# A 1x1 convolution's first image by seven half-size products for eight, in a two-layer convolution kernel on one core

## The chip, the cores and the metric

The kernel runs on one core of a Trainium2 chip. A core has a matrix engine (TensorE, PE in the profile), a vector engine (VectorE, DVE), a scalar engine (ScalarE, ACT), a general engine (GpSimd, POOL) and a queue engine (SyncE, SP). Each takes its instructions in order; they wait for each other on semaphores. DMAs are issued from SP, ACT or POOL. The metric is the device time of one execution in microseconds, lower is better.

## The reference

The input x has 4 images of 1024 channels and 56 x 56 pixels, float32. Two layers follow each other. The change is in the first line of the first layer, for the first image.

```
# layer 0
r = relu(conv1x1(x, w1) + b1)                 # 1024 -> 256 channels
off = conv3x3(r, w_off) + b_off               # 18 offsets a pixel
s = bilinear samples of r at 9 taps moved by off
r = relu(einsum(s, w2) + b2)                  # 256 -> 256
x = relu(x + conv1x1(r, w3) + b3)             # 256 -> 1024
# layer 1
out = relu(bn(conv1x1(x, w1)))                # 1024 -> 256, statistics over the batch
out = relu(bn(conv3x3(out, w2)))
out = bn(conv1x1(out, w3))                    # 256 -> 1024
return relu(x + softplus(residual_scale) * out)
```

## The kernel before

Channels lie on the 128 partitions, pixels along the free axis. An image is cut into 7 blocks of 8 rows, 448 pixels (BLK), which stage_a takes one by one. For block j of image n:

- load_x (L252, L254) loads x in four pieces of 256 channels into the pool xin, which has four buffers. So a piece for the next block is loaded when the same piece of this block has been used.
- The first product (L266) is 8 groups of input channels by 2 halves of output channels, 16 matmuls 448 wide, into acc, a PSUM tile of two banks with one buffer. Each float32 matmul is two instructions in the profile, so that a block shows 32.
- Two ScalarE operations (L278) read acc, add the bias, apply relu and write feat.
- From the third block on, stage_b of the block two before comes in between: po (L355) turns the offsets on PE, and 16 small VectorE operations (L368 to L390) make sampling weights and indices.
- pm (L292) is the offset convolution, part (L301) its copy by VectorE, and six small DMAs (L309) on SP bring it into offc.
- ftp (L322) turns feat on PE, three ScalarE copies (L329 to L332) fill ft, and four DMAs (L336, L340) on SP store it into the image's table in memory, twice, for two corners of a sample.

When image 0 has all seven blocks, its sampling begins: an indirect DMA on GpSimd (L405) gathers rows of the table into one of the eight buffers g of the pool gat, ScalarE (L415) and VectorE (L417) mix four corners, PE turns the result (stp, L439) and multiplies it (L455). From here on the blocks of the next image and the last products (stage_c, L480 and L507) are woven in by a budget of columns. Image 0's blocks have nothing to be woven with; they run one after another, followed by image 1's first product.

The kernel is written against a scheduling layer: it places buffers, orders each engine's instructions by its own estimates, and puts in the semaphore waits. Two details matter here. The order on an engine need not be that of the source. And every DMA from SP or ACT takes one of eight semaphores in turn, so that a DMA can be issued only when an earlier one with the same semaphore has landed.

Of the kernel before, what the change touches and what calls it, by code (L numbers as in the profile page):

```python
# [8 lines left out]
F32 = mybir.dt.float32  # L9
I32 = mybir.dt.int32  # L10
AF = mybir.ActivationFunctionType
ALU = mybir.AluOpType

N, CIN, H, W = 4, 1024, 56, 56
CB = 256
KC = CIN // 128
KB = CB // 128
HW = H * W
ROWS = 8
BLK = ROWS * W  # L20
NJ = H // ROWS
# [17 lines left out]
R2S = 5  # L39
X1S = 6  # L40
# [20 lines left out]
def deform_bottleneck_then_bn_bottleneck(  # L61
# [15 lines left out]
    nc = tc.nc  # L77
# [23 lines left out]
    def col(name, k):  # L101
        c = COLS[name] + k
        return ch[:, c : c + 1]
# [64 lines left out]
    with ExitStack() as l0:  # L168
# [4 lines left out]
        xin = l0a.enter_context(tc.tile_pool(name="xin", bufs=4, side="right"))  # L173
        worka = l0a.enter_context(tc.tile_pool(name="work_a", bufs=2, side="right"))
        xres = l0.enter_context(tc.tile_pool(name="xres", bufs=2))
        gat = l0.enter_context(tc.tile_pool(name="gat", bufs=8))
        work = l0.enter_context(tc.tile_pool(name="work", bufs=2))
        w3p = l0.enter_context(tc.tile_pool(name="work3", bufs=3))
        per_image = l0.enter_context(tc.tile_pool(name="per_image", bufs=2))
        ps1 = l0.enter_context(tc.tile_pool(name="ps1", bufs=4, space=bass.MemoryType.PSUM))  # L180
        ps2 = l0.enter_context(tc.tile_pool(name="ps2", bufs=1, space=bass.MemoryType.PSUM))

        w1 = wa.tile([128, KC, CB], F32, tag="w1", name="w1")
# [12 lines left out]
        def load_later():  # L196
            nc.sync.dma_start(w2, a_w2.rearrange("(h p) t o -> p h t o", p=128))
            nc.sync.dma_start(w3, a_w3.rearrange("(h p) o -> p h o", p=128))
            nc.sync.dma_start(c1w, b_w1.rearrange("(k p) o -> p k o", p=128))
# [26 lines left out]
        def load_zeros():  # L226
            zero = w3p.tile([128, CB], F32, tag="s", name="zero", bufs=12)
            nc.vector.memset(zero[: PW + 2], 0.0)
            for n in range(N):
                for corner, s in enumerate((0, PW)):  # L230
                    first_row = PW - s + TPAD
                    for r0, r1 in ((0, first_row), (first_row + H * PW, TROWS)):
                        if r1 > r0:
                            nc.sync.dma_start(tables[n][r0:r1, corner, :], zero[: r1 - r0, :])

        feats = []
        for i in range(2):
            f = wa.tile([128, KB, ROWS, PW], F32, tag=f"feat{i}", name=f"feat{i}")
# [7 lines left out]
        xts = {}  # L246

        def load_x(n, j, kk):
            if n == N:
                return  # L250
            if (n, j) == (0, 0):
                nc.sync.dma_start(w1[:, kk : kk + 2], w1_v[:, kk : kk + 2])  # L252
            xt = xin.tile([128, 2, BLK], F32, tag="xt", name=f"xt_{n}_{j}_{kk}")
            nc.sync.dma_start(xt, x_v[n, :, kk : kk + 2, j * BLK : (j + 1) * BLK])  # L254
            xts[n, j, kk] = xt

        def stage_a(n, j):

            b = n * NJ + j
            acc = ps2.tile([128, KB, 512], F32, tag="wide", name=f"acc1_{b}")
            for k in range(KC):
                xt = xts.pop((n, j, k)) if k % 2 == 0 else xt
                for h in range(KB):
                    nc.tensor.matmul(  # L266
                        acc[:, h, :BLK],
                        w1[:, k, h * 128 : (h + 1) * 128],
                        xt[:, k % 2, :],
                        start=(k == 0),  # L270
                        stop=(k == KC - 1),
                    )
                if k % 2:
                    load_x(*((n, j + 1) if j + 1 < NJ else (n + 1, 0)), k - 1)
                yield KB * BLK
            f = feats[b % 2]
            for h in range(KB):
                nc.scalar.activation(  # L278
                    f[:, h, :, 1 : 1 + W],
                    acc[:, h, :BLK].rearrange("p (r w) -> p r w", w=W),  # L280
                    AF.Relu,
                    bias=col("a_b1", h),
                )
            if j > 1:
                yield from stage_b(n, j - 2)
            yield None


            pm = ps1.tile([128, BLK], F32, tag="bank", name=f"pm_{b}")
            for kj in range(3):  # L290
                for h in range(KB):
                    nc.tensor.matmul(  # L292
                        pm[64 * h : 64 * h + 64, :],
                        woff[:, h, kj, :],
                        f[:, h, :, kj : kj + W],
                        start=(kj == 0),
                        stop=(kj == 2),
                    )
            yield 3 * BLK
            part = worka.tile([128, BLK], F32, tag="part", name=f"part_{b}")  # L300
            nc.vector.tensor_copy(part, pm)  # L301

            for ki in range(3):
                y0, y1 = ROWS * j + 1 - ki, ROWS * (j + 1) + 1 - ki
                lo, hi = max(y0, 0), min(y1, H)
                for h in range(KB):
                    to = (3 * h + ki) * OFFS
                    at = 64 * h + ki * OFFS
                    nc.sync.dma_start(  # L309
                        offc[to : to + OFFS, lo * W : hi * W],  # L310
                        part[at : at + OFFS, (lo - y0) * W : (hi - y0) * W],
                    )

            ft = worka.tile([128, QFULL + 1, CB], F32, tag="ft", name=f"ft_{b}")
            for half in range(2):
                tp = ps1.tile([128, 2, CB], F32, tag="bank", name=f"ftp_{b}_{half}")
                for i in range(2):
                    t = 2 * half + i
                    m = 128 if t < QFULL else QREST
                    for h in range(KB):  # L320
                        fv = f[:, h].rearrange("p r w -> p (r w)")
                        nc.tensor.transpose(  # L322
                            tp[:m, i, h * 128 : (h + 1) * 128],
                            fv[:, t * 128 : t * 128 + m],
                            ident,
                        )
                yield CB
                if half == 0:
                    nc.scalar.copy(ft[:, 0:2, :], tp)  # L329
                else:  # L330
                    nc.scalar.copy(ft[:, 2, :], tp[:, 0, :])
                    nc.scalar.copy(ft[:QREST, 3, :], tp[:QREST, 1, :])  # L332
            q = PW * (ROWS * j + 1)
            for corner, s in enumerate((0, PW)):
                r = q - s + TPAD
                nc.sync.dma_start(  # L336
                    tables[n][r : r + QFULL * 128, corner, :].rearrange("(t p) c -> p t c", p=128),
                    ft[:, :QFULL, :],
                )
                nc.sync.dma_start(  # L340
                    tables[n][r + QFULL * 128 : r + QB, corner, :], ft[:QREST, QFULL, :]
                )

# [257 lines left out]
        for kk in range(0, KC, 2):  # L601
            load_x(0, 0, kk)
# [13 lines left out]
        for j in range(NJ):  # L616
            for _ in stage_a(0, j):
                pass
            if j == 1:
                load_later()  # L620
            if j == 3:
                load_zeros()
# [20 lines left out]
        def next_stage(n, passed):  # L643
            if first_ones and first_ones[0][0] == n + 1:
                if first_ones[0][1] <= passed * (NJ + 1) or not last_ones:
                    running.append(stage_a(*first_ones.pop(0)))
                    return running[-1]
            if last_ones:
                return stage_c(*last_ones.pop(0))
            return None  # L650
# [50 lines left out]
    with l1:  # L701
# [8 lines left out]
        v, vs = [], []  # L710
        for p in range(6):
            t = wino.tile([128, QUADS, KB, PW], F32, tag=f"v{p}", name=f"v{p}")
# [273 lines left out]
        for i, p in [(i, p) for i in range(len(parts)) for p in SEQ] + [(len(parts), None)]:  # L986
            begun = begin(i, p) if p is not None else None
            if before is not None:
                j, q, _ = before
# [19 lines left out]
    ps2 = ctx.enter_context(tc.tile_pool(name="ps2_l1", bufs=1, space=bass.MemoryType.PSUM))  # L1009
# [30 lines left out]
    with ExitStack() as l2:  # L1040
# [46 lines left out]
        first = ps1.tile([128, 512], F32, tag="bank", name="first")  # L1087
        for h in range(KB):
# [4 lines left out]
                start=True,  # L1093
                stop=True,
# [5 lines left out]
        for i in range(0, len(chunks), 2):  # L1100
            n, at, m = chunks[i + 1]
# [71 lines left out]
    for n in range(N):  # L1173
        for j in range(NJ):
            blk = slice(j * BLK, (j + 1) * BLK)
            for kk in range(0, KC, 2):
                x1t = fin.tile([128, 2, BLK], F32, tag="x1f", name=f"x1f_{n}_{j}_{kk}")
                nc.sync.dma_start(x1t, x1_v[n, :, kk : kk + 2, blk])
                last = (n, j, kk) == (N - 1, NJ - 1, KC - 2)
                for d in range(2):  # L1180
                    k = kk + d
# [68 lines left out]
```

## Time and profile before

| | us |
|---|---|
| median of 3 runs | 2911.69 |
| lowest, highest | 2909.29, 2919.39 |
| the profiled execution | 2925.49 |
| its span, first to last instruction | 2923.6 |
| mean granted clock of TensorE | 0.990 of full |

The profile counts from the span's start. PE is busy for 98% of it and VectorE for 64%. The stretches below are block by block; the columns are the stretch, its length, then the busy time and number of instructions of PE, of weight loads on PE, of VectorE, ScalarE and GpSimd, then PE's granted clock, the DMA engines' busy share and GB/s.

```profile
0.00:25.16 25.16, 17.85 (x52) 9.04 (x53) 10.24 (x49) 4.37 (x7) 0.79 (x7) 1.00 0.83 295
25.16:41.93 16.77, 16.04 (x54) 8.16 (x53) 0.63 (x1) 2.28 (x6) 0.00 (x0) 1.00 0.71 236
41.93:58.76 16.83, 16.42 (x58) 8.63 (x57) 3.58 (x16) 2.24 (x6) 0.00 (x0) 1.00 0.73 242
58.76:75.60 16.84, 16.43 (x59) 8.64 (x58) 3.58 (x16) 2.29 (x6) 0.00 (x0) 1.00 0.60 186
75.60:95.49 19.89, 16.58 (x58) 8.56 (x57) 3.58 (x16) 3.21 (x8) 0.00 (x0) 1.00 0.52 170
95.49:114.05 18.56, 18.14 (x57) 9.46 (x58) 3.58 (x16) 1.35 (x3) 0.00 (x0) 0.91 0.69 218
114.05:130.88 16.83, 16.33 (x57) 8.54 (x56) 3.32 (x16) 2.28 (x6) 0.00 (x0) 1.00 0.57 177
130.88:147.71 16.83, 12.19 (x34) 5.89 (x32) 0.50 (x2) 2.60 (x6) 5.23 (x6) 0.97 0.72 226
```

Each stretch is one block of image 0, from one first product's start to the next; the last holds image 1's first product and the start of the sampling. Matmuls overlap in their pipeline, and a record of one is longer (0.55 us at 448 wide) than the time from one to the next. A lone matmul's record is thus no measure of the pace.

### The profile page before, as it was taken

Reading aid. Unit: us, or ns where it says so; the run is one execution under the profiler, and the core shown is the slowest. Engines: PE = TensorE matmul, PEld = TensorE weight load, DVE = VectorE, ACT = ScalarE, POOL = GpSimd, SP = SyncE. Lnnn points to the kernel's source line nnn. Section 1 sums busy time; section 2 is a strip of 40 time slices with the busy share of each in tenths; the row PEclk is TensorE's granted clock in tenths of the full one; section 3 lists DMA queues with packets and bytes.
Section 4 is the critical chain, followed back from the end, with each engine's and each line's share of the span. In section 5 each row is a group of like instructions: output and inputs, shape, how many; then the busy total and the mean of one; then the engine's idle time right before and its main releaser. Section 6 shows DMA issues by size and latency. Waiting matters only on the chain. (4 is left out here: it accounts for less than half of the span.)

```text
span 2923.6 us, 34375 instructions
## 1 busy us (share of the span) xinstructions
PE 2852.8 (98%) x10473; PEld 1700.7 (58%) x10473; DVE 1884.1 (64%) x4257; ACT 1188.6 (41%) x2439; POOL 1029.2 (35%) x998
## 2 busy tenths in 40 slices
PE   8899999999999999999999899999989998999999
PEld 4444455565554555555555455545669998965554
DVE  2188676676566667666676786767659887344444
ACT  1144443444334444344344344444434544334444
POOL 0065554456445546555554654444300000000000
PEclk9999999999999999999999999999999999999999
DMA  7699999898898999888897999999731101049997
GB/s 249 192 382 387 334 330 318 301 357 313 301 339 304 337 300 347 313 316 327 321 337 232 366 324 311 333 334 320 234 101 46 46 23 64 14 159 311 308 308 261
DMA packets 330331, 789.49 MB, mean 270 GB/s; under 512 B 31352, under 2 KB 176800, under 8 KB 329888
## 3 DMA queue, kind: packets, MB, share of 16 engines
q0 software_dynamic: 127296, 462.48, 44.4%
q1 hardware_dynamic: 172368, 273.41, 27.8%
q10 hardware_dynamic: 30480, 51.39, 4.7%
q8 instruction: 83, 1.36, 0.2%
q14 instruction: 104, 0.85, 0.1%
HBM read 639.11 MB, written 142.70 MB: 267 GB/s over the span
## 5 line engine op out<-in xcount | busy, mean ns | idle before, releaser
L405 POOL DMA_INDIRECT g<-table,idxs x900 | 1018.3, 1131 | 1080.8 <-DVE s L417 550.9
L417 DVE SCALAR_TENSOR_TENSOR s<-g,wts,s 128x256 f32<-128x256 f32 (+1 forms) x2700 | 1134.1, 478 | 344.3 <-ACT s L415 326.7
L455 PE MATMUL acc<-sts,w 128*128 128x512 f32 (+2 forms) x2016 | 809.0, 543 | 0.6 <-ACT r L465 0.6
L415 ACT ACTIVATE s<-g,wts 128x256 f32<-128x256 f32 x900 | 417.7, 509 | 469.4 <-PE stp L439 370.6
L455 PEld LDWEIGHTS acc<-sts,w 128*128 128x128 f32 x2016 | 363.0, 191 | 281.4 <-issue 197.4
L507 PE MATMUL pr<-r,w 128*128 128x512 f32 (+2 forms) x896 | 371.0, 545 | 13.0 <-DVE x1t L514 6.6
L480 PE MATMUL acc<-x1t,c1w 128*128 128x512 f32 (+2 forms) x896 | 370.1, 542 | 5.7 <-ACT x1t L517 5.7
L266 PE MATMUL acc<-xt,w 128*128 128x448 f32 x896 | 355.0, 547 | 14.1 <-DMA xt<-in_x_dram 9.5
L1018 PE MATMUL pf<-y,c3w 128*128 128x448 f32 x844 | 317.4, 539 | 0.0
L517 ACT ACTIVATE x1t<-x1t 128x512 f32<-128x512 f32 (+2 forms) x224 | 128.7, 575 | 446.2 <-DVE x1t L514 430.9
L514 DVE SCALAR_TENSOR_TENSOR x1t<-pr,ch,xr 128x512 f32<-128x512 f32 (+2 forms) x224 | 151.9, 681 | 226.8 <-PE pr L507 169.0
L439 PEld LDWEIGHTS stp<-ident,s 128*128 128x128 f32 (+1 forms) x1800 | 213.8, 142 | 139.6 <-issue 89.0
L266 PEld LDWEIGHTS acc<-xt,w 128*128 128x128 f32 x896 | 170.5, 193 | 173.7 <-issue 161.3
L480 PEld LDWEIGHTS acc<-x1t,c1w 128*128 128x128 f32 x896 | 171.2, 191 | 171.7 <-issue 117.3
L507 PEld LDWEIGHTS pr<-r,w 128*128 128x128 f32 x896 | 170.4, 192 | 172.5 <-issue 105.1
L439 PE MATMUL stp<-ident,s 128*128 128x128 f32 (+1 forms) x1800 | 248.1, 274 | 9.8 <-ACT sts L445 4.7
L445 ACT COPY sts<-stp 128x512 f32<-128x512 f32 (+2 forms) x504 | 243.1, 527 | 33.6 <-PE stp L439 33.6
L1182 DVE SCALAR_TENSOR_TENSOR x1f<-pf,sc_bn,x1f 128x448 f32<-128x448 f32 x211 | 144.3, 684 | 172.4 <-PE pf L1018 147.0
L1018 PEld LDWEIGHTS pf<-y,c3w 128*128 128x128 f32 x844 | 160.4, 190 | 156.8 <-issue 118.9
L1190 ACT ACTIVATE x1f<-x1f,sh_bn 128x448 f32<-128x448 f32 x224 | 148.3, 667 | 173.7 <-DVE x1f L1182 172.8
L845 PE MATMUL q<-v,u 128*128 128x196 f32 x576 | 109.5, 337 | 10.9 <-DVE v L797 9.7
L845 PEld LDWEIGHTS q<-v,u 128*128 128x128 f32 x576 | 99.4, 191 | 15.6 <-ACT y L762 10.2
(195 smaller groups left out, 1754.4 us busy)
## 6 DMA issues: line engine op xcount, KB each, us to landing
xt<-in_x_dram SPq DMA_DIRECT2D x112, 448.0 KB
x1f<-x_d SPq DMA_DIRECT2D x112, 448.0 KB
out_dram<-x1f ACTq DMA_DIRECT2D x111, 448.0 KB
xr<-in_x_dram SPq DMA_DIRECT2D x64, 512.0 KB
x_d<-x1t SPq DMA_DIRECT2D x128, 256.0 KB
table<-ft SPq DMA_DIRECT2D x56, 384.0 KB
g<-table,idxs POOLq DMA_INDIRECT x900, 7.2
xr<-in_x_dram SPq DMA_DIRECT2D x32, 384.0 KB
```

The costliest lines, as they stand in the source:

```text
L266: nc.tensor.matmul(acc[:, h, :BLK], w1[:, k, h * 128 : (h + 1) * 128], xt[:, k % 2, :], start=(k == 0), stop=(k == KC - 1),)
L405: nc.gpsimd.indirect_dma_start(out=g[:m], out_offset=None, in_=tables[n].rearrange("r q c -> r (q c)"), in_offset=bass.IndirectOffsetOnAxi ...
L415: nc.scalar.activation(s[:m], g[:m, 0:CB], AF.Copy, scale=wt[:, 0])
L417: nc.vector.scalar_tensor_tensor(s[:m], g[:m, corner * CB : (corner + 1) * CB], wt[:, corner], s[:m], ALU.mult, ALU.add,)
L439: nc.tensor.transpose(banks[h][:, t * 128 : t * 128 + m], s[:m, h * 128 : (h + 1) * 128], ident[:m, :m],)
L445: nc.scalar.copy(sts[:, h, :size], banks[h][:, :size])
L455: nc.tensor.matmul(acc[:, o, :size], w2[:, h, k, o * 128 : (o + 1) * 128], sts[:, h, :size], start=(k == 0 and h == 0), stop=(k == TAPS - ...
L480: nc.tensor.matmul(acc3[:, h, :size], c1w[:, k, h * 128 : (h + 1) * 128], x1t, start=(k == 0), stop=(k == KC - 1),)
L507: nc.tensor.matmul(pr, w3[:, h, k * 128 : (k + 1) * 128], r2[:, h, :size], start=(h == 0), stop=(h == KB - 1),)
L514: nc.vector.scalar_tensor_tensor(x1t, pr, col("a_b3", k), xr[:, d, :], ALU.add, ALU.add)
L845: nc.tensor.matmul(ps[:, o].rearrange("p r c -> p (r c)"), wt, x, start=first and j == 0 and (alone or o == 0), stop=last and j == len(pai ...
L1018: nc.tensor.matmul(pz, c3w[:, h, k * 128 : (k + 1) * 128], y2[n][:, h, j * BLK : (j + 1) * BLK], start=(h == 0), stop=(h == KB - 1),)
```

## The change

For blocks 1 to 6 of image 0 the first product is split in halves: the 8 groups of input channels into two times 4, the 256 output channels into two times 128, and the 448 pixels into two times 224. Eight products of half sizes become seven, by Winograd's form of Strassen's scheme: four sums of weights, made once by VectorE after the first block, and four sums of x a block, eight VectorE instructions of 448 elements. The seven products, 4 matmuls 224 wide each, go into three places of acc: y and z in one bank, v in the other. ScalarE reads a partial result of y or v into feat between products (keep), VectorE adds another one to it (finish), and ScalarE applies relu. Block 0 and the other images keep 16 matmuls.

With it, image 0's x goes into the eight buffers of the samples (gat), so that a block's x is loaded while the block before is computed, and the table stores of image 0 are issued from ScalarE's queue and no longer from SP's. The sums of x lie in buffers of r2, the sums of weights in buffers of x1t, both unused until image 0's samples are multiplied.

```diff
-            xt = xin.tile([128, 2, BLK], F32, tag="xt", name=f"xt_{n}_{j}_{kk}")
+            if n == 0:
+                xt = gat.tile([128, 4 * CB], F32, tag="g", name=f"xt_{n}_{j}_{kk}")
+                xt = xt[:, : 2 * BLK].rearrange("p (k q) -> p k q", k=2)
+            else:
+                xt = xin.tile([128, 2, BLK], F32, tag="xt", name=f"xt_{n}_{j}_{kk}")
...
+        def sums_of_weights():
+            for i in range(4):
+                t = w3p.tile([128, 512], F32, tag="x1t", name=f"w1_{i}", bufs=X1S)
+                w1_sums.append(t.rearrange("p (k o) -> p k o", k=half_k))
+            s1, s2, s3, s4 = w1_sums
+            nc.vector.tensor_add(s1, a21, a22)
+            nc.vector.tensor_sub(s2, s1, a11)
+            nc.vector.tensor_sub(s3, a11, a21)
+            nc.vector.tensor_sub(s4, a12, s2)
+
+        def seven(j, acc, f):
+            for kk in range(0, KC, 2):
+                load_x(*following(0, j), kk)
...
+            for i in range(2):
+                ks = slice(2 * i, 2 * i + 2)
+                lo, hi = x[i], x[i + 2]
+                nc.vector.tensor_sub(t1[:, ks], lo[:, :, n1], lo[:, :, n0])
+                nc.vector.tensor_sub(t2[:, ks], hi[:, :, n1], t1[:, ks])
+                nc.vector.tensor_sub(lo[:, :, n1], hi[:, :, n1], lo[:, :, n1])
+                nc.vector.tensor_sub(t4[:, ks], hi[:, :, n0], t2[:, ks])
...
+            y, z, v = acc[:, 0, :half_n], acc[:, 0, 256 : 256 + half_n], acc[:, 1, :half_n]
...
+            def keep(h, at, t):
+                nc.scalar.activation(place(h, at), rows(t), AF.Identity, bias=col("a_b1", h))
+
+            def finish(h, at, t):
+                nc.vector.tensor_add(place(h, at), place(h, at), rows(t))
+                nc.scalar.activation(place(h, at), place(h, at), AF.Relu)
+
+            times(y, a11, part(0, n0), True)
+            keep(0, 0, y)
+            times(v, s1, chunks_of(t1), True)
+            keep(1, 1, v)
+            times(y, s2, chunks_of(t2))
+            keep(0, 1, y)
+            times(z, a12, part(2, n0))
+            finish(0, 0, z)
+            times(y, s3, part(0, n1))
+            finish(1, 1, y)
+            times(v, s4, part(2, n1))
+            finish(0, 1, v)
+            times(y, a22, chunks_of(t4))
+            nc.scalar.activation(place(1, 0), rows(y), AF.Relu, bias=col("a_b1", 1))
...
+            if n or j == 0:
+                yield from eight(n, j, acc, f)
+            else:
+                yield from seven(j, acc, f)
...
+            queue = nc.sync if n else nc.scalar
...
-                nc.sync.dma_start(
+                queue.dma_start(
                     tables[n][r : r + QFULL * 128, corner, :].rearrange("(t p) c -> p t c", p=128),
```

The function times issues the four matmuls of a product; eight is the loop of before, in a function of its own, with image 0's loads for the next block ahead of it.

## The prediction

> **What bounds the kernel now.** I read the page first, then the timeline of TensorE over the first 150 us, the busy time by stretch, the groups by shape, and the order of instructions with their waits in both built programs. From the page:
>
> ```profile
> PE 2852.8 (98%) x10473; PEld 1700.7 (58%) x10473; DVE 1884.1 (64%) x4257; ACT 1188.6 (41%) x2439; POOL 1029.2 (35%) x998
> ```
>
> PE is busy nearly throughout, and the sampling of image 0 starts only when its seven blocks are done. So time gained or lost on PE in the first 148 us moves everything behind it. The timeline of PE, blocks 1, 3, 5 and the step to image 1:
>
> ```profile
> 25.16 12.19 PE L266 MATMUL acc<-xt,w 128*128 128x448 f32 x32
> ...
> 38.08 2.99 PE L292 MATMUL pm<-feat,woff 128*64 128x448 f32 x12 [0.73 <-ACT feat L278]
> ...
> 58.76 12.19 PE L266 MATMUL acc<-xt,w 128*128 128x448 f32 x32
> 70.79 0.54 PE L355 MATMUL po<-ident,offc 108*128 108x108 f32 x4
> 71.74 3.00 PE L292 MATMUL pm<-feat,woff 128*64 128x448 f32 x12 [0.41 <-ACT feat L278]
> ...
> 95.49 13.91 PE L266 MATMUL acc<-xt,w 128*128 128x448 f32 x32 [2.90 <-DMA xt<-in_x_dram]
> ...
> 147.71 3.35 PE L266 MATMUL acc<-xt,w 128*128 128x448 f32 x4 [4.64 <-ACT feat L278]
> ```
>
> A product of 16 matmuls is 32 instructions here. From its start to pm's start takes 12.92 us in block 1 and 12.98 in block 3 (po within); I use 12.96. Their pace is (12.19 - 0.55 of the last one) / 31 = 0.3755 us, so 32 take 12.02, and the one stop for ScalarE's read of PSUM costs 12.92 - 12.02 = 0.90: the 0.73 shown plus 0.17 of pipelining lost. A block repeats every 16.8 us. Block 5 also waits 2.90 for x, and its product runs 13.91 - 12.19 = 1.7 longer. The stretches say why:
>
> ```profile
> 91.00:94.50 3.50, 1.59 (x11) 0.84 (x8) 1.05 (x6) 1.12 (x3) 0.00 (x0) 1.00 1.03 379
> 94.50:98.00 3.50, 2.51 (x4) 1.31 (x5) 0.00 (x0) 0.00 (x0) 0.00 (x0) 0.63 0.23 72
> 143.50:147.00 3.50, 0.00 (x0) 0.00 (x0) 0.00 (x0) 0.98 (x2) 2.79 (x3) 0.94 0.92 303
> 147.00:150.50 3.50, 2.79 (x4) 1.40 (x5) 1.94 (x4) 1.17 (x3) 2.58 (x4) 0.50 1.01 373
> ```
>
> (us, then busy time of PE, weight loads, DVE, ACT, POOL, then PE's clock.) Where PE worked under half of a stretch, the next has a clock of 0.63 or 0.50.
>
> Prices for the new work, from the groups with shapes kept apart:
>
> ```profile
> L845 PE MATMUL q<-v,u 128*128 128x196 f32 x576 | 109.5, 337 | 10.9 <-DVE v L797 9.7 <-ACT y L883 0.9
> L278 ACT ACTIVATE feat<-acc,ch 128x448 f32<-128x448 f32 x56 | 32.6, 631 | 159.8 <-PE acc L266 159.8
> L872 ACT ACTIVATE y<-q,ch 128x196 f32<-128x196 f32 x16 | 6.1, 436 | 56.1 <-PE q L845 56.1
> L895 DVE TENSOR_TENSOR y<-y,b 128x392 f32<-128x392 f32 x24 | 13.4, 559 | 5.6 <-ACT y L883 2.8 <-PE b L845 2.3
> ```
>
> and from the timeline of PE in layer 1's 3x3 product:
>
> ```profile
> 2251.27 2.87 PE L845 MATMUL q<-v,u 128*128 128x196 f32 x16
> ...
> 2253.97 1.54 PE L845 MATMUL b<-v,u 128*128 128x203 f32 x8
> ```
>
> There 16 instructions 196 wide took 2.70 us (2251.27 to 2253.97), 0.169 each. Narrow matmuls keep the pace of their columns; the weight load does not bind.
>
> **What the Trainium skill says.** "TensorE: Matmul & The Clock Gate", section on the HAM clock gate: an idle window of about 3.4 us halves the clock until a busy one has passed. The stretches above agree (0.50 after 3.5 us without a matmul). "PSUM — Partial Sum Buffer", section on bank collisions: guard PSUM by bank and quadrant, not by address. No run here shows a collision, but it explains why halves of one bank can't be written and read at once. "Trainium Kernel Development and Optimization", Key Constraints: DMAs of SP and ACT share the 16 engines, so another queue saves only issue time. In the trace that is real: six offc issues hold SP 4.5 us before the table stores.
>
> **The change part by part.** *Columns.* Blocks 1 to 6 (block 0 stays): 7x4 matmuls of 224, 56 instructions; at 0.19 (between 0.3755/2 and 0.169x224/196 = 0.193) 10.6 us against 12.02: -1.4 a block.
>
> *Waits.* The scheduler puts a wait between every product and the next. v's product waits for ScalarE's read of y, the next for the read of v, z's for the second read of y; the last three each wait for VectorE's add of the product before. Six stops a block, though y, z and v lie apart. ScalarE's half-size read: 436 ns + 28 columns at (524 - 436)/124 ns from the 320-column row = 0.46 us; VectorE's: 559 ns less 168 columns at 1.04 = 0.38. Stops: 0.90 - 0.63 + 0.46 = 0.73 and 0.90 - 0.63 + 0.38 = 0.65. Three of each: 4.1 us. pm's first matmul no longer waits; the second does, behind 0.24 us of work: 0.5. po's 0.43 falls into these stops. Sum 10.6 + 4.1 + 0.5 = 15.2 against 12.96: +2.2 a block, +13.4 for six. Bounds of a stop: below 0.17 (lost pipelining alone) it can't fall; 0.90 is the full-size one.
>
> *What stands in front of these readers.* DVE gets eight sums of x a block (448 elements, 0.62 us: 4.9 us), 2.7 us of weight sums once and three adds. In DVE's order, block 2's first add stands behind sums that need the last x of block 3; that load is behind six offc issues on SP (landing about 8.5 us after pm, plus 1.5 us of sums, against 8.9 when needed: +1.0), and its second behind 11 small operations of stage_b at 0.23 (2.5 us against 1.5: +0.9). In blocks 4 to 6 po now stands after the second product and needs offc of the block just before. In block 1 the last offc landed 6.5 us after pm's end (47.57 against 41.07); the second product is done at 0.9 (ftp) + 1.5 + 0.7 + 1.5 = 4.6. It waits 1.9 instead of 0.73, plus 0.3 of po: +1.4 each. Together +6; bounds 0 to 14, since ScalarE's table stores stand ahead of its next reads and wait for earlier DMAs whose semaphores they share.
>
> *x.* Loads for the next block are issued a block ahead, into the samples' tiles, so the 2.90 wait and the 1.7 of slow clock go: -4.6 (bounds 0 and -4.6). The samples need these tiles after block 6; their first gather waits for the tables anyway.
>
> *Table stores.* Off SP, image 0's last stores are issued about 4 us earlier after the last transposes, so the first gather, now 10.1 us after image 1's first product starts (140.96 - 130.88), comes at about 6.5, the first scaled sample at 12.2 instead of 15.8. But ScalarE's order now has three samples ahead of image 1's feat (one before), and PE's next product waits for feat: 18.5 us against 16.8, less four transposes done meanwhile (0.9): +0.8, taken as +1; bounds -3.5 and +4. After that PE's order is unchanged.
>
> Sum: 13.4 + 6 - 4.6 + 1 = +15.8 us. The profiled execution had a span of 2923.6 and lasted 2925.49; it becomes about 2941. It was 13.8 over the median of the runs shown; the same difference on 2911.69 gives 2927.5, +0.54%.
>
> **Rivals.**
> *B, the stops breed longer ones.* PE rests 30% of each section; with a further wait of 2 us a stretch falls under half busy and the clock drops. Two stretches of 3.4 us at half speed a block are 3.4 us, 20 for six: 2948. For it: the clock rows above. Against: stretches 70 to 80% busy kept 1.00.
> *C, faster: the reads are short enough.* It happens in the six stops: a block gains 12.96 - 10.6 - 0.5 = 1.86 with no stops, so below 0.31 us a stop the product gains. With all hidden: -11.2 - 4.6 - 3.5 = -19: 2892. For it: only a quarter of a product's time separates it from being covered, if the waits were satisfied earlier than named. Against: the next product waits for the read of the one just ended, so nothing covers it, and 0.73 us for such a read stands in the trace.
> *D, no change.* Stops of 0.5 and no further waits: 6x(10.6 + 3.0 + 0.5 - 12.96) = +6.8, less 4.6: 2914.
>
> **How the numbers follow.** Forecast 0.58 (own range 2920 to 2938), B 0.17, C 0.10, D 0.15. 0.3% is 8.7 us, about what can be told from no change. Slower holds most of the forecast, B and little of D: 0.75; within: 0.15; faster: 0.10. The range 2913 to 2948 takes in D's and B's centres and leaves C out.
>
> **What would show it.** In the changed profile: 28 half-width matmuls a block, paced at 0.19 an instruction; between groups of eight instructions an idle of 0.5 to 0.6 us ended by ACT feat or DVE feat in turn; a section from first product to pm of about 15 us, 16 to 17 where po waits for offc; no wait for x in block 5; the first gather 6 to 7 us after image 1's first product starts; the last block ending some 15 us later. It is wrong if these idles are under 0.3 us, or if the stretches show a clock of 0.5 to 0.8 through the section (B).

## The result

The changed kernel is slower by about three times what was forecast.

| us | before | changed |
|---|---|---|
| median of 6 runs each | 2914.51 | 2962.57 |
| lowest, highest | 2909.29, 2919.39 | 2949.85, 2967.65 |
| span of the profiled execution | 2923.6 | 2961.6 |
| image 1's first product starts | 130.88 | 169.18 |

The ratio is 1.0158, 95% interval 1.0132 to 1.0183, or +48 us between the medians; 2927.5 and at most 2948 had been said. Between the two traces 38.3 us are there when image 1 starts, and 38.0 are left at the end of the span. So the loss lies in image 0's blocks. The busy time by stretch, one block of image 0 a line, from one first product to the next (start and end, length, PE, weight loads, VectorE, ScalarE, GpSimd, PE's clock, the DMA engines' share, GB/s):

```profile
25.30:50.04 24.74, 18.91 (x78) 13.96 (x77) 5.09 (x11) 4.09 (x11) 0.00 (x0) 0.86 0.75 254
50.04:71.97 21.93, 16.61 (x82) 12.71 (x81) 7.92 (x26) 4.08 (x11) 0.00 (x0) 1.00 0.43 136
71.97:104.26 32.29, 20.38 (x83) 15.50 (x82) 13.04 (x34) 4.09 (x11) 0.00 (x0) 0.79 0.62 212
104.26:125.79 21.53, 16.54 (x82) 12.63 (x81) 9.35 (x28) 4.08 (x11) 0.00 (x0) 1.00 0.43 139
125.79:147.39 21.60, 16.70 (x83) 12.63 (x82) 6.15 (x22) 4.09 (x11) 0.00 (x0) 1.00 0.17 53
147.39:169.18 21.79, 16.52 (x82) 12.59 (x81) 4.49 (x19) 4.09 (x11) 0.00 (x0) 1.00 0.17 53
```

No block reaches the 16.8 us of before. Four take 21.5 to 21.9, block 1 takes 24.7 and block 3 takes 32.3, and these two have a clock below 1. PE's timeline shows the start of the bad block (the third), and a plain one (the fifth):

```profile
71.97 1.68 PE L341 MATMUL acc<-xt,w 128*128 128x224 f32 x8
73.49 0.35 PE L460 MATMUL po<-ident,offc 108*128 108x108 f32 x2
83.53 3.36 PE L341 MATMUL acc<-t,w 128*128 128x224 f32 x8 [9.69 <-ACT feat L353]
87.42 3.36 PE L341 MATMUL acc<-t,w 128*128 128x224 f32 x8 [0.54 <-ACT feat L353]
...
125.79 1.68 PE L341 MATMUL acc<-xt,w 128*128 128x224 f32 x8
127.31 0.26 PE L460 MATMUL po<-ident,offc 108*128 108x108 f32 x1
129.37 1.78 PE L341 MATMUL acc<-t,w 128*128 128x224 f32 x8 [1.80 <-ACT feat L353]
132.19 0.62 PE L460 MATMUL po<-ident,offc 108*128 108x108 f32 x3 [1.04 <-DMA offc<-part]
132.65 1.70 PE L341 MATMUL acc<-t,w 128*128 128x224 f32 x8
134.88 1.78 PE L341 MATMUL acc<-xt,w 128*128 128x224 f32 x8 [0.54 <-ACT feat L353]
137.22 1.78 PE L341 MATMUL acc<-xt,w 128*128 128x224 f32 x8 [0.55 <-DVE feat L356]
139.48 1.78 PE L341 MATMUL acc<-xt,w 128*128 128x224 f32 x8 [0.48 <-DVE feat L356]
141.74 1.78 PE L341 MATMUL acc<-t,w 128*128 128x224 f32 x8 [0.48 <-DVE feat L356]
143.45 3.08 PE L395 MATMUL pm<-feat,woff 128*64 128x448 f32 x12
```

Seven groups of eight instructions are the seven products, and between them stand the forecast's stops, 0.48 to 0.55 us of idle. The surprise is the first stop. It is 1.80 in block 5 and 9.69 in block 3, where the next two products then run at half pace, 3.36 us for 1.78. All six first stops are long; what they wait for is ScalarE's first read. ScalarE's own timeline in block 3 shows what it did instead:

```profile
72.48 0.38 ACT L435 COPY ft<-ftp 80x256 f32<-80x256 f32 x1
73.13 0.37 ACTq L441 DMA_DIRECT2D table<-ft  x1
76.76 0.32 ACTq L445 DMA_DIRECT2D table<-ft  x1
80.10 0.37 ACTq L441 DMA_DIRECT2D table<-ft  x1
82.66 0.32 ACTq L445 DMA_DIRECT2D table<-ft  x1
83.03 0.45 ACT L353 ACTIVATE feat<-acc,ch 128x224 f32<-128x224 f32 x1 [10.17 <-DMA table<-ft]
```

The product was ready at about 73.5, but the read is the fifth in ScalarE's queue, behind four table stores of the block before. Each issue takes only 0.3 to 0.4 us; the time between them is waiting. By the built program the four wait for the semaphores of, in turn, a zero store into image 3's table, a piece of x of block 4, another zero store and a piece of x of image 1, all issued on SP. The trace shows the last two landings: the zero store issued at 69.85 lands at 80.08, the x issued at 72.89 at 82.64. Each takes about 10 us, with the DMA engines at 1.01 from 72 to 76 us. So traffic had its part in the length of these waits, and the order of the queue put ScalarE's read behind them. SP's timeline shows how late these DMAs were issued:

```profile
55.80 11.74 SPq L234 DMA_DIRECT2D table<-zero  x11
67.64 2.16 SPq L259 DMA_DIRECT2D xt<-in_x_dram  x4
69.85 0.62 SPq L234 DMA_DIRECT2D table<-zero  x1
70.52 2.73 SPq L259 DMA_DIRECT2D xt<-in_x_dram  x2
```

The zero stores pad the tables of all four images; each goes out only when an earlier DMA with the same semaphore has landed, and eleven of them hold SP for 11.7 us.

### The profile page after: what moved, and what is told of

It reads as the page before. It is cut to its first block, busy times and chain, and to the rows that moved or that the text cites. A ratio compares the mean times of both kernels' runs of the same rounds, so it can differ in the third digit from the quotient of the medians.

```text
span 2961.6 us, 34761 instructions
## 1 busy us (share of the span) xinstructions
PE 2859.7 (97%) x10617; PEld 1728.7 (58%) x10617; DVE 1920.4 (65%) x4327; ACT 1200.2 (41%) x2469; POOL 1028.5 (35%) x998
## 5 line engine op out<-in xcount | busy, mean ns | idle before, releaser
L274 PE MATMUL acc<-xt,w 128*128 128x448 f32 x704 | 278.9, 544 | 7.4 <-DMA xt<-in_x_dram 6.6
L544 PE MATMUL stp<-ident,s 128*128 128x128 f32 (+1 forms) x1800 | 248.3, 274 | 15.2 <-ACT sts L550 6.0
L274 PEld LDWEIGHTS acc<-xt,w 128*128 128x128 f32 x704 | 133.4, 192 | 132.8 <-issue 126.1
```

What stands on the lines that cost most here:

```text
L274: nc.tensor.matmul(acc[:, h, :BLK], w1[:, k, h * 128 : (h + 1) * 128], xt[:, k % 2, :], start=(k == 0), stop=(k == KC - 1),)
L544: nc.tensor.transpose(banks[h][:, t * 128 : t * 128 + m], s[:m, h * 128 : (h + 1) * 128], ident[:m, :m],)
```

## The experiments

Two readings stood against each other. *Q* (queue): the stores stand in ScalarE's order ahead of a read that PE waits for; put them elsewhere and 24 us come back. *T* (traffic): x, weights and zeros fill the DMA engines earlier, and someone waits wherever the stores are issued. Ten kernels were run. The table has image 0's blocks 1 to 6 from one first product to the next (a wait for x counts in the block before it), the start of image 1's first product, the median, and the ratio to runs of before on the same chip with its 95% interval (it need not be the ratio of the medians).

| kernel | blocks 1 to 6, us | image 1 | median | ratio |
|---|---|---|---|---|
| before | 16.8 16.8 16.8 19.9 18.6 16.8 | 130.9 | 2914.5 | 1 |
| changed | 24.7 21.9 32.3 21.5 21.6 21.8 | 169.2 | 2962.6 | 1.0158 (1.0132 to 1.0183) |
| st_sp | 19.4 19.5 19.8 22.3 19.7 19.6 | 146.4 | 2930.9 | 1.0043 (1.0028 to 1.0059) |
| no_seven | 16.8 16.8 16.8 17.1 16.8 16.8 | 126.0 | 2914.3 | 1.0000 (0.9985 to 1.0014) |
| two_tiles | 18.4 15.8 16.7 28.4 15.3 15.7 | 135.7 | 2928.7 | 1.0043 (1.0030 to 1.0056) |
| two_tiles_sp | 13.9 17.9 17.1 26.3 18.2 14.7 | 133.7 | 2918.8 | 1.0015 (1.0002 to 1.0027) |
| zeros_pool | 27.8 21.9 26.3 21.2 22.4 21.9 | 167.4 | 2955.1 | 1.0135 (1.0116 to 1.0154) |
| best1 | 13.9 17.8 15.9 14.7 14.7 14.7 | 118.1 | 2904.1 | 0.9966 (0.9952 to 0.9980) |
| best3 | 13.9 14.6 14.7 14.7 15.0 14.7 | 121.4 | 2909.8 | 0.9984 (0.9973 to 0.9995) |
| x_only | 16.8 16.8 16.8 19.3 18.6 16.8 | 131.4 | 2915.1 | 1.0001 (0.9991 to 1.0010) |
| best2 | 13.9 14.6 14.7 14.9 15.1 14.7 | 114.2 | 2897.0 | 0.9929 (0.9912 to 0.9946) |
| st_act_only | 16.8 16.8 20.9 16.8 16.8 16.8 | 130.0 | 2918.0 | 1.0010 (0.9995 to 1.0025) |

Runs of one kernel on one chip differ by up to 27 us, and the medians do not follow the starts of image 1 exactly. The starts are the finer measure of what happens in image 0, the ratios of the whole.

**st_sp: the stores back on SP.**

```diff
-            queue = nc.sync if n else nc.scalar
+            queue = nc.sync
```

> The changed kernel with image 0's table stores issued from SP again; seven products and x's double buffering stay. In the changed kernel image 1's first product starts at 169.2 us, 38.3 later than before (130.9). Theory Q (queue): the four stores stand in ScalarE's order ahead of the first read of the next block's product, by 2.4 us of issue and in block 3 by 10 us of waiting for earlier DMAs; that costs 18 us at the first stop of the six blocks and breeds 6 us of halved clock. Then this kernel's image 1 starts at about 145, block 3 is as long as blocks 4 to 6, and the time is about 14 us above before (2928). Theory T (traffic): image 1's x, the weights and the zeros are loaded earlier and fill the DMA engines, and someone waits for them wherever the stores are issued. Then block 3 stays near 30 us, the wait moves to x or offc, and the time stays above 2950.

Image 1 starts at 146.4, block 3 is as long as blocks 1, 2, 5 and 6, and the clock is 1.00 in all six; block 4 is longer by two waits, for offc and for VectorE. Q holds: 22.8 us of the 38.3 come, in the balance, from issuing four DMAs a block from ScalarE and not from SP. ScalarE's timeline in block 3:

```profile
66.88 0.45 ACT L353 ACTIVATE feat<-acc,ch 128x224 f32<-128x224 f32 x1 [0.85 <-PE acc L341]
69.26 0.45 ACT L353 ACTIVATE feat<-acc,ch 128x224 f32<-128x224 f32 x1 [1.93 <-PE acc L341]
```

The read now waits for PE and PE for it in turn, which is the forecast's picture.

**no_seven: the change without its seven products.** Sixteen matmuls in all blocks, the rest as changed.

```diff
-            if n or j == 0:
+            if True:
                 yield from eight(n, j, acc, f)
...
-            if j == 0:
-                sums_of_weights()
```

> The changed kernel with sixteen matmuls in every block: x double-buffered in the samples' tiles and stores on ScalarE's queue, no seven products. Theory Q: ScalarE reads a product only at its end, 12 us after it starts, so the stores ahead of it are covered (even block 3's 10 us); the x wait of block 5 goes. Image 1 starts 4 to 5 us earlier than before, at 126 to 127, and the time is 4 to 8 us below before. Theory T: block 3 is longer than 20 us here too, and the time is above before.

Image 1 starts where expected, at 126.0: a product of 12 us hides everything that ScalarE does ahead of its read, and the wait for x is gone. The same stall is there: in block 4 the four stores are issued between 77.29 and 86.42 us, and the read at 87.58 still waits for PE alone. The median did not follow, so that half of the expectation missed. The trace shows where the gain went. From image 1's start to the 202nd of the 2016 instructions of the product with w2 takes 241.4 us here and 236.5 before, so that this instruction starts at 367.3 us here and 367.4 before.

**two_tiles: z and v in a tile of their own.** The scheduler makes each product wait for the read of the one just before because all three places are one tile. The tile of the tap sums is free until image 0 is sampled.

```diff
-            y, z, v = acc[:, 0, :half_n], acc[:, 0, 256 : 256 + half_n], acc[:, 1, :half_n]
+            other = ps2.tile([128, KB, 512], F32, tag="tap", name=f"zv_{j}")
+            y, z, v = acc[:, 0, :half_n], other[:, 0, :half_n], other[:, 1, :half_n]
...
-            times(z, a12, part(2, n0))
+            times(z, a12, part(2, n0), True)
```

> The changed kernel with z and v in a PSUM tile of their own (that of the tap sums, unused until image 0 is sampled), so that no product waits for the read of the one just ended; stores stay on ScalarE. Theory Q with stops of 0.75 to 0.8 us each: the stops go except for the first read, which the stores still delay, by 0.6 us a block and 8 to 12 us in block 3. Image 1 starts at about 131 to 135, the time is within 5 us of before. If instead the stops cost nothing because the chain of ScalarE and VectorE reads sets the pace, under half of the 15 us that the stops make up comes back, and image 1 starts after 160.

PE's timeline, the fifth block:

```profile
104.75 1.68 PE L342 MATMUL acc<-xt,w 128*128 128x224 f32 x8
106.27 1.68 PE L342 MATMUL zv<-t,w 128*128 128x224 f32 x8
107.78 0.26 PE L461 MATMUL po<-ident,offc 108*128 108x108 f32 x1
108.34 1.78 PE L342 MATMUL acc<-t,w 128*128 128x224 f32 x8 [0.29 <-ACT feat L354]
109.95 1.68 PE L342 MATMUL zv<-xt,w 128*128 128x224 f32 x8
```

Products follow each other at 1.51 us with no idle between most of them; the stops were the price of sharing a tile. ScalarE's queue still stalls one block, here the fourth, by 10.4 us with slow products after it. The start of image 1 is just outside the expected 131 to 135. The median is 14 us above before where 5 were said; the profiled execution was the fastest of its runs (2915.92), so the trace does not show what the others lost.

**two_tiles_sp: both steps.**

> Both: z and v in a tile of their own, stores from SP again. Theory Q and the stops: a section from first product to offset convolution of about 11 us for 12.96, no stop over 0.3 us besides that at the offsets; image 1 starts at 114 to 118, and the time is 12 to 16 us below before (about 2900). If VectorE's eight sums a block or x's arrival set the pace instead, the sections stay above 14 us and the time is not below before.

It missed, although four of the blocks ran as was said or faster (9.98 to 11.06 us from first product to offset convolution). Two blocks waited for x, which the expectation had named as what else might set the pace:

```profile
57.41 1.02 PE L342 MATMUL acc<-xt,w 128*128 128x224 f32 x4 [2.93 <-DMA xt<-in_x_dram]
...
100.78 1.86 PE L342 MATMUL acc<-xt,w 128*128 128x224 f32 x4 [11.36 <-DMA xt<-in_x_dram]
```

SP's timeline names the cause. The four loads of block 5 come after the table stores and all twelve zero stores:

```profile
81.08 12.20 SPq L234 DMA_DIRECT2D table<-zero  x12
93.38 3.16 SPq L259 DMA_DIRECT2D xt<-in_x_dram  x4
```

With faster blocks, x is needed sooner, and an in-order queue in which it stands last is the new bound. T has a grain of truth, then, but more about a queue than about bandwidth. The next kernels test that.

**zeros_pool: the changed kernel, zeros from GpSimd's queue.**

```diff
-                            nc.sync.dma_start(tables[n][r0:r1, corner, :], zero[: r1 - r0, :])
+                            nc.gpsimd.dma_start(tables[n][r0:r1, corner, :], zero[: r1 - r0, :])
```

> The changed kernel, stores still on ScalarE, but the twelve stores of zeros (57 to 59 rows each, which pad the tables) issued from GpSimd and no longer from SP. In the changed kernel block 3's four table stores are issued at 73.1, 76.8, 80.1 and 82.7, and by the program each waits on the semaphore of a zero store or of an x load queued behind the zero stores. Theory L (shared semaphores): with the zeros off SP these earlier DMAs land some 10 us sooner, block 3's first stop is under 4 us instead of 10, its clock stays at 1.00, block 3 lasts 22 to 24 us instead of 32.3, image 1 starts at 157 to 161, and the time falls by 8 to 12 us against the changed kernel (about 2951). Rival W (bandwidth): the DMA engines are full at 70 to 77 us, so the stores wait whatever queue the zeros have; block 3 stays above 28 us.

ScalarE's timeline in block 3:

```profile
76.30 0.37 ACTq L441 DMA_DIRECT2D table<-ft  x1
76.76 1.03 ACTq L445 DMA_DIRECT2D table<-ft  x1
77.83 0.53 ACTq L441 DMA_DIRECT2D table<-ft  x1
79.91 0.32 ACTq L445 DMA_DIRECT2D table<-ft  x1
80.27 0.45 ACT L353 ACTIVATE feat<-acc,ch 128x224 f32<-128x224 f32 x1 [3.74 <-DMA table<-ft]
```

The stop shrinks from 9.69 to 3.26 us, as shared semaphores say and bandwidth does not: the DMA engines were about as busy from 68 to 76 us (0.96 and 0.97 by halves, 0.80 and 1.01 in the changed kernel). What is left is the fourth store's wait for the first one of the same block (76.30 to 79.88), for a block's six DMAs of offsets and four stores go around the eight semaphores more than once. But 3.26 is still long enough here for the next two products to run at half pace, so block 3 takes 26.3 and not 22 to 24, and block 1, with three products at half pace for one, gives back 3.0 of the 6.0 us that block 3 gained. Image 1 starts at 167.4 and the median is 2955.1, both outside what was expected.

**best1 and best3: two tiles, stores on SP, zeros on GpSimd; in best3 the later weights too.** best1 is two_tiles_sp with the edit of zeros_pool; best3 adds this for each of the three loads in load_later:

```diff
-            nc.sync.dma_start(w2, a_w2.rearrange("(h p) t o -> p h t o", p=128))
+            nc.gpsimd.dma_start(w2, a_w2.rearrange("(h p) t o -> p h t o", p=128))
```

> z and v in a tile of their own, table stores on SP, zeros on GpSimd. With the zeros on SP this kernel waited 11.4 us for x in block 5, because x's loads stood behind the zero stores on SP (12.2 us of issues), and 2.9 us in block 3 behind two weight loads of 1 MB, each with about 3 us of halved clock. Theory L: block 5's wait goes, block 3's stays; image 1 starts at 118 to 121 and the time is about 8 to 12 us below before. Rival W: the engines are full, x comes late anyhow, waits over 4 us stay in blocks 4 to 6, and the time is not below before.

> The same with the weights of the later stages (4.4 MB) loaded from GpSimd's queue too. Theory L: SP's queue holds x's loads alone besides offsets and table stores, block 3's wait for x goes as well, all six blocks last 14 to 15 us, image 1 starts at 113 to 117, and the time is 12 to 16 us below before. Rival W: the weights take the same engines at the same time, block 3 keeps its wait of about 3 us.

best1 did what was said: block 5's wait is gone, block 3's of 2.83 us stays. In best3 that one goes too and all six blocks take 13.9 to 15.0 us. Yet image 1 starts later, and the start and the time (4.7 us below before) both miss what was expected. On GpSimd's queue, where nothing was ahead of them, the weights went out at 1.57 us and shared the DMA engines with w1 and the first x. The first two pieces of x were issued at 2.13 and 3.16 us in both kernels, but the first product began at 12.49 us for 6.63 and stopped once more for 1.79. Here traffic does cost, at the one place where PE has nothing else to do.

**x_only: before, with x double-buffered alone.** The diff's load_x and eight, sixteen matmuls in every block, all stores on SP.

> Before with x double-buffered in the samples' tiles alone: sixteen matmuls in every block, all stores on SP. If double buffering does what it is for, the wait for x in block 5 (2.9 us, and 1.7 of slow clock) goes and image 1 starts 4 to 5 us earlier than before, at 126 to 127. If x's loads queued behind the stores and zeros on SP come late here too, as in the kernel with both tiles, one block waits for x by more than 2 us and image 1 starts at 129 or later.

The second case came: block 5 still waits 2.28 us, because its loads stand behind six zero stores (83.71 to 88.07 on SP). Two sets of buffers for x gain nothing while its loads queue behind something slow. In no_seven, with the table stores off SP, the wait is gone.

**best2: best1 with the weights later.** They stay on SP, and in the program they stand behind block 3. The scheduling layer still issues w2 at 22.21 us (22.29 in best1); w3 and the weights of layer 1 go out at 63.74 and 76.23 us for 46.91 and 47.80.

```diff
-            if j == 1:
+            if j == 3:
                 load_later()
```

> z and v in a tile of their own, table stores on SP, zeros on GpSimd as before, and the two later weight loads of 1 MB each moved behind block 3, so that block 3's x no longer stands behind them on SP. Theory L: block 3's wait of 2.8 us for x and the half-used section after it go (block 3 lasted 19.1 us for 14.7 in blocks 4 to 6), the wait does not come back elsewhere, image 1 starts at 113.5 to 115 and the time is about 15 us below before (2899). If the weights only move the wait to block 4 or 5, image 1 starts at 118 or later and the time is that of the kernel without this step.

The stretches of blocks 3 and 4:

```profile
54.89:69.57 14.68, 14.68 (x82) 13.05 (x81) 9.84 (x31) 4.09 (x11) 0.00 (x0) 1.00 0.75 249
69.57:84.43 14.86, 14.85 (x82) 13.01 (x81) 7.22 (x33) 4.26 (x11) 0.00 (x0) 1.00 0.69 225
```

PE is busy throughout both, as in blocks 1 and 2 (13.92 of 13.92 us and 14.63 of 14.63), and the wait for x in block 3 is gone: its loads are issued from 46.89 us on, with no weights in front of them. Image 1 starts at 114.2, 55 us earlier than in the changed kernel, and the time beats both kernels: 2897.0 us, 0.7% below before.

**st_act_only: before, with image 0's table stores issued from ScalarE.**

> Before with image 0's table stores issued from ScalarE alone: sixteen matmuls, x in its own buffers. Theory Q: ScalarE has 12 us of product in which to issue, so the blocks keep their 16.8 us and image 1 starts at 130 to 132. The three samples that stand ahead of image 1's relu in ScalarE's order then cost 3 to 5 us within the first tenth of the products with w2, as in the other kernels with these stores, although the first gather comes 3 to 4 us earlier. If that loss came from the x in the samples' tiles instead, the first tenth ends within 1 us of before.

Image 1 starts at 130.0 as expected, by two errors that cancel. Block 3 stopped 3.16 us for offsets and ran its offset convolution in 4.06 us for 3.0, and in return the wait for x in block 5 went. The stores of block 3 lasted until 72.37 us, so that ScalarE's read came 1.4 us later in its block than in block 2: a product of 12 us does not cover every such stall. After image 1's start, 241.1 us pass until the 202nd instruction with w2, 4.6 more than before, although the first gather comes at 136.7 and not 141.0. So this loss does not need x in the samples' tiles. The five kernels with these stores on ScalarE need 2.6 to 4.8 us more than before for this stretch, those with them on SP between 0.4 less and 3.7 more. So the loss is there, but the two groups overlap; that it comes from the samples in ScalarE's order is argued and not shown.

## Why the prediction was wrong

*Columns and stops: right.* A plain block's products come at 2.32 us after a read by ScalarE, and at 2.33 and then twice 2.26 after one by VectorE, each with 1.51 of work: stops of 0.81 and 0.75 for 0.73 and 0.65 forecast. The offset convolution follows the last product after 1.71 us, so its stop is 0.20 for 0.5. The section is 3 x 2.32 + 2.33 + 2 x 2.26 + 1.71 = 15.52 us for 15.2. Over six blocks that is +15.4 against the +13.4 of the sum. That y, z and v lie apart did not help, as it said: two_tiles removed the stops by nothing but another tile.

*What stands in front of these readers: the step that failed.* It was taken as +6 with bounds 0 to 14. The trace holds 27.1:

- The first stop of each block. From the first product to the second take 4.93, 3.59, 11.56, 3.63, 3.58 and 4.64 us, 2.32 being the plain distance: 18.0 too much. The prediction named the table stores ahead of ScalarE's reads, and put them into the bound alone. It gave no price to their issue, about 2.4 us for four of them (50.69 to 53.08 in block 2), and none to the wait for semaphores that they share with SP's loads and zeros. It held that another queue saves only issue time; here the move cost waits, 22.8 us in the balance. st_sp shows what issue and waits cost together, and zeros_pool that the long wait of block 3 hangs on SP's zeros.
- The halved clock that follows, in blocks 1 and 3: 2.7 and 3.6 us by the same distances, 6.3. This is rival B, in two blocks of six and not in all.
- Offsets and VectorE's queue: 1.2 in block 2, where an add stood behind a sum that waited 2.96 us for x, and 0.8 and 0.9 in blocks 4 and 5, where po waited for offc: 2.9 with rounding. This is what the prediction had counted in detail, and had put at 6.

*x: the right number, and not by the reason given.* The wait and the slow clock in block 5 went, 4.9 us for 4.6. x_only shows that double buffering alone did not do it. The wait also went in st_act_only, where x has its old buffers and the table stores are off SP, and in st_sp, where they are on SP and the blocks last 19.4 us and more.

*Table stores and the first gather: half right.* The first gather comes 6.6 us after image 1's start (175.81 and 169.18), the first scaled sample after 12.1; 6 to 7 and 12.2 were said. The cost up to the 202nd instruction with w2 is +3.3 (239.8 for 236.5), within its bounds but above the +1 that was taken.

Together 15.4 + 27.1 - 4.9, and 0.6 for the rest of the blocks (3.94 for 3.84 us six times), make 38.2 of the 38.3 us. Without the stores on ScalarE the kernel's ratio is 1.0043, next to the forecast's +0.54%: the seven products were priced nearly right and the plain line at the end of the diff was not. That these two agree so closely is in part luck, for st_sp has 3.2 us in front of its readers where 6 were forecast, and 1.1 us that it lost before block 1. Of the 48 us between the medians some 10 lie behind image 0, or in the chance of the profiled executions (before's was 11 us above its median). What they are stays open.

## What to carry to other kernels

When a DMA moves to a compute engine's queue, price it there: its issue and its waits stand ahead of the next instruction of that engine, and what counts is how soon another engine needs that instruction. The same four stores were covered under a 12 us product in no_seven and cost 23 us in six blocks under products of 1.5 us. An order of short accumulations needs its places in tiles that the scheduler tells apart, and a second set of buffers helps only as far as the loads into it are not last in their queue.

## What the runs showed of the hardware

- The wait for a DMA's semaphore is taken by the queue that issues the next DMA, and everything behind it there stands still: 10.17 us of ScalarE for stores that took 0.3 to 0.4 us to issue. The Trainium skill says so ("DMA: Bandwidth & Descriptors", section on the anatomy of one DMA: a semaphore wait happens on the issuing sequencer, the DMA engines do not wait), and the trace agrees.
- The clock does not fall at one fixed length of idle. Stops of 3.16, 3.24, 3.26 and 9.69 us were followed by slow products, and so were one of 2.28 in x_only (13.96 us for 12.19) and one of 2.07 in block 5 of zeros_pool (2.44 us for 1.78), while stops of 2.83 (best1), 2.87 and 2.95 (block 6 of the changed kernel and of zeros_pool) were not.
- What counts is PE's share of work in fixed steps of time. In each of the twelve traces all changes of the clock lie on one grid of 3.413 us: in the changed kernel at 10.32, 30.80, 37.62, 78.58 and 92.24 us, 6, 2, 12 and 4 steps apart. Over the twelve traces, all 100 steps that began at full clock and had PE busy for under 45% were followed by a halved clock, 3 of 34 between 45 and 50%, and 1 of 9887 above. Three such steps, of x_only, best1 and the changed kernel's block 6 (the first number after the length is PE's busy time):

```profile
93.57:96.98 3.41, 1.13 (x4) 0.68 (x4) 0.00 (x0) 0.85 (x3) 0.00 (x0) 1.00 0.67 232
53.52:56.93 3.41, 1.80 (x13) 1.08 (x10) 1.70 (x10) 1.12 (x3) 0.00 (x0) 1.00 1.08 370
150.26:153.67 3.41, 1.64 (x9) 1.57 (x10) 0.00 (x0) 0.45 (x1) 0.00 (x0) 1.00 0.66 210
```

The clock fell at the end of the first and not of the others, so a stop's place on the grid decides along with its length. The Trainium skill ("TensorE: Matmul & The Clock Gate", section on the HAM clock gate) says that the window of about 3.4 us runs free, and the grid agrees. It speaks of an idle window; here one with PE busy for 1.34 of 3.41 us was enough (zeros_pool, up to 127.96 us).

- Twelve small stores of zeros held SP's queue for 11 to 13 us where they stood in one row (11.05 in two_tiles, 13.32 in st_sp). Issued from GpSimd, which was idle, they left PE busy throughout blocks 1 to 4 in best2.
